# Local attention with a routed feed-forward layer on one core: weighing and joining moved behind the next scores

## The chip, the core and the metric

The kernel runs on one core of a Trainium2 chip. The core has five engines that run their own instruction streams in order and meet at semaphores: TensorE (matrix products; the profile calls its matmuls PE and its weight loads PEld), VectorE (DVE), ScalarE (ACT), GpSimd (POOL) and SyncE (SP, which here issues DMAs). TensorE writes to PSUM[...]; VectorE and ScalarE read it from there.

The metric is the device time of one launch in microseconds (us). Before the change it is 582.45 us, the median of three runs (581.14 to 582.88).

## The reference

The input x is 2 sequences of 2048 tokens with 256 channels. One block is computed:

```python
x = L0_attn_x                                            # (2, 2048, 256)
x = _layernorm(x + _L0_attn_ref(x, W_attn, b_attn, W_proj, b_proj))
x = _layernorm(x + _L0_ffn_ref(x, Wr, W1, b1, Wo, bo, gamma, beta))
```

The attention has 16 heads of 16 channels; a token sees itself and the 64 tokens before it (scores of other tokens are minus infinity), then softmax, weighted values, and the projection W_proj. The feed-forward part sends each token to the one of 8 experts with the largest router logit (`argmax` of softmax(x @ Wr.T)), computes gelu(x @ W1[e] + b1[e]) with 1024 hidden units, multiplies by the shared Wo, adds bo and x, and normalises with gamma and beta.

## The kernel before

The 4096 tokens are 32 tiles of 128. Four tiles make a chunk of 512, whose q, k and v are projected together. The kernel has two stages: the attention with the routing (one loop over 32 tiles, and an epilogue), and then blocks of 128 tokens of one expert each, gathered by indirect DMA, with a weight matrix of 1 MB per block.

The order of the work is written out by hand: `manual_schedule` keeps on every engine the order in which the Python code issues instructions. The loop is a software pipeline. In iteration i four tiles are in work: t = i, u = i - 1, w = i - 2 and z = i - 3.

- `scores(t)` (L533, L545): the mask and 64 small matmuls per tile, into four PSUM banks s0 to s3 that exist once each. The scores of the next tile therefore wait until the exponentials of this tile have read their bank.
- `row_max(t, r)` (VectorE, L557) and `exps(t, r)` (ScalarE, L561, four instructions) for each bank r.
- `fold(t, pair)` (GpSimd, L573, L581), `inverse` (VectorE, L589, L594), `spread_inverse` (GpSimd, L602): the sums of the softmax and their reciprocals.
- `turn(u, r)` (TensorE, L616): the probabilities are transposed, 128x128 four times per r. `keep_turned` copies them to SBUF, r = 0 and 2 on ScalarE (L622), r = 1 and 3 on VectorE (L624).
- `weigh(u)` (TensorE, L636, 64 narrow matmuls): the weighted values. `keep_weighed` (ScalarE, L646) copies them.
- `turn_inverse(w)` (TensorE, L655) and `normalise(w)` (VectorE, L659).
- `join(w)`: the output projection (TensorE, L667), the sum with the residual (VectorE, L673) and its statistics (L676, L677). `norm_scale(z)` (GpSimd, L683, L684) and `norm(z)` (VectorE, L692, which also stores the result) finish the first layer norm. `turn_x1`, `keep_x1` (L705, L710), `route` (L717, L722) and `turn_logits` (L727, L728) compute the router's logits, once per four tiles.
- Two slots per iteration hold the projections of later chunks: `project` (TensorE, L422, L426, L433) and `keep` (ScalarE L469, L475, L489; VectorE L471, L480, L483, L494, L499). By the slots the tiles are of some kinds. Tiles 6, 10, 14, 18, 22 transpose x and project q; 5, 9, ..., 25 project q and k with ScalarE draining both; 7, 11, ... hold k, v and the routing; 8, 12, ... a transposition of x and v. In the light tiles 1, 3 and 26 to 28 each slot is half a projection, and from tile 29 the first slot is empty; there the second exponentials come behind the second copy of turned probabilities.

PSUM has three pools. The score banks are one. The second, `turned`, has two buffers that alternate over all calls of `turn`, `turn_inverse`, `turn_x1`, `join`, `route`, `turn_logits`, `rank` and `table`: each waits until the one two calls earlier has been read. The third, `psum`, has two buffers for projections and weighted values.

The order of the parts in one iteration before the change, on TensorE: scores(t), turn(u, 0), turn(u, 1), first slot, turn(u, 2), turn(u, 3), second slot, turn_inverse(w), weigh(u), turn_x1(z), join(w). On ScalarE: copy of turn 0, exps 0 and 1, copy of turn 2, the first slot's copy, exps 2, the second slot's copy, exps 3, keep_weighed, keep_x1.

Small VectorE operations that sort tokens into lots (`hot`, `rank`, `places`) and that list the first blocks (`first_blocks`) are spread over iterations through the dictionary `early`. `full` marks iterations in which they are issued ahead of the first slot's projection.

Of the kernel before, what the change touches and what calls it, by code (L numbers as in the profile page):

```python
# [21 lines left out]
TPC = CH // P  # L22
NEG = -1.0e30
GAP = 64
SPLIT = (0, 8, 16, 28, 32)
PIECES = 8
WARM = 16
EARLY = 2
# [5 lines left out]
def kernel(  # L34
# [19 lines left out]
    KC = C // P  # L54
# [237 lines left out]
    with ExitStack() as att:  # L292
# [32 lines left out]
        def load_rest():  # L325
            nc.sync.dma_start(out=wpj, in_=w_proj.rearrange("(k p) f -> p k f", p=P))
            nc.sync.dma_start(out=bp_bc, in_=b_proj.partition_broadcast(P))
# [112 lines left out]
        def prepare(c, piece):  # L440

            first = c % (TPB // TPC) == 0
            if piece == 0:
                axT[c] = p2.tile([P, KC, CH], F32, tag="xT", name=f"xT_{c}")
            elif piece == 1:
                qs[c] = p2.tile([P, KC, 2, CH], F32, tag="q", name=f"q_{c}")
            elif piece == 2:
                ks[c] = p2.tile([P, KC, CTX + CH], F32, tag="k", name=f"k_{c}")
                if first:
                    nc.gpsimd.memset(ks[c][:, :, 0:CTX], 0.0)  # L450
                else:
                    nc.gpsimd.tensor_copy(ks[c][:, :, 0:CTX], ks[c - 1][:, :, CH : CH + CTX])
            else:

                vs[c] = values[c % 2]
                if c < 2:
                    nc.gpsimd.memset(
                        vs[c][:, :, :, 1, :].rearrange("p j m d -> p (j m) d"), 0.0
                    )

                vh[c] = p2.tile([P, TPC, NH // 2, 3, HD], F32, tag="h", name=f"h_{c}")
                if first:
                    nc.gpsimd.memset(vh[c][0:CTX, 0].rearrange("p m s d -> p (m s d)"), 0.0)
# [194 lines left out]
        def normalise(i):  # L658
            nc.vector.tensor_tensor(avs[i], avs[i], rTs.pop(i)[:, 0:KC, :], ALU.mult)  # L659

        def join(i):
            c, j = divmod(i, TPC)
            av = avs.pop(i)
            py = turned(f"py_{i}")
            py = py.rearrange("p a b -> p (a b)")
            for k in range(KC):
                nc.tensor.matmul(  # L667
                    py[:, 0:C], lhsT=av[:, k, :], rhs=wpj[:, k, :],
                    start=(k == 0), stop=(k == KC - 1),
                )  # L670

            s = xbs[c][:, j, :]
            nc.vector.tensor_tensor(s, py[:, 0:C], s, ALU.add)  # L673
            st = small.tile([P, 6], F32, tag="st", name=f"st_{i}")
            mv = small.tile([P, 2], F32, tag="mv", name=f"mv_{i}")
            nc.vector.bn_stats(st, s)  # L676
            nc.vector.bn_aggr(mv, st)  # L677
            norms[i] = mv
# [444 lines left out]
        xts[1] = load_x(1)  # L1123
        for n in range(3):
            prepare(0, n)
            for part in range(2):
                project(0, n, part)
                keep(0, n, part)
            if n == 0:
                load_rest()  # L1130

        def quick_sums(i, r):

# [53 lines left out]
        def put(at, *call, to=plan):  # L1187
            to.setdefault(at, []).append(partial(*call))


        for n, (t0, t1) in enumerate(lots[:EARLY]):
            at = t1 + 4
            put(at, some, ("hot", n), 3, to=early)
            put(at + 1, rest, ("hot", n), to=early)
            put(at + 2, rank, n, to=early)
            put(at + 2, some, ("places", n), 1, to=early)
            put(at + 3, some, ("places", n), 3, to=early)
            put(at + 4, rest, ("places", n), to=early)
            for t in range(t0, t1, 2):
                spread[at + 5 + (t - t0) // 2] = [partial(one_hots, nc.gpsimd, t)]  # L1200
        for n, count in enumerate((1, 4, 4, 4, 3)):
            put(SPLIT[EARLY] + 8 + n, some, "first", count, to=early)
        put(SPLIT[EARLY] + 13, rest, "first", to=early)
        for n in range(4 * (NT - 27)):
# [3 lines left out]
        for i in range(NT):  # L1208
# [4 lines left out]
            if w is not None:  # L1213
                inverse(w)
            scores(t)
            if z is not None and z > 0 and z % TPC == 0:
                route(z // TPC - 1)
            row_max(t, 0)
            if i == 0:
                consts = routing_constants()  # L1220
                for r in range(1, 4):
                    row_max(t, r)
                for r in range(2):
                    exps(t, r)
                for n in ((0, 3), (1, 0), (1, 1)):
                    prepare(*n)
                for part in ((0, 3, 0), (0, 3, 1), (1, 0, 0), (1, 0, 1)):
                    project(*part)
                    keep(*part)
                add_bias(0)  # L1230
                xts[2] = load_x(2)
                for r in range(2, 4):
                    exps(t, r)
                for part in parts[:2]:
                    project(*part)
                    keep(*part)
                for pair in range(2):
                    fold(t, pair)
                continue
            if i == 3:  # L1240
                turn_router()
            if u is not None:
                turn(u, 0)
                keep_turned(u, 0)
                turn(u, 1)
            if z is not None:
                norm_scale(z)
            if w is not None:
                spread_inverse(w)
            for part in slots:  # L1250
# [1 line left out]
                    prepare(*part[:2])  # L1252
            exps(t, 0)
            row_max(t, 1)
            if u is not None:
                keep_turned(u, 1)


            full = slots[0] and slots[1] and slots[0][1] > 0 and slots[0][3] == (0, 1)
            full = full or i == SPLIT[EARLY] + 8 or i >= NT - 4  # L1260
            if full:
                for task in early.get(i, ()):
                    task()
# [35 lines left out]
            exps(t, 2)  # L1299
            if slots[1]:  # L1300
                project(*slots[1][:4])
            if w is not None:
                turn_inverse(w)
                normalise(w)
            if t == NT - 1:
                for b in range(2):
                    gather(b)
# [7 lines left out]
                keep(*slots[1][:4])  # L1315
            elif slots[1] and slots[1][3][-1] == 1:
                keep(*slots[1][:3])
            if u is not None:
                weigh(u)
            exps(t, 3)  # L1320
            if t < NT - 1:
                fold(t, 1)
            if u is not None:
                keep_weighed(u)
            if i == NT - 2:
                table(0)
            if z is not None:
                turn_x1(z)
                keep_x1(z)

            if i == TPC:
                load_experts()
            if i == 2 * TPC:
                turn_biases()
            for task in plan.get(i, ()):
                task()
            if t == NT - 1:
                quick_sums(t, 1)
            if w is not None:
                join(w)  # L1340

        u, w, z = NT - 1, NT - 2, NT - 3
        lot = len(lots) - 2
        tiles = list(range(*lots[lot]))
        norm_scale(z)
        for n in range(4 * (NT - 27), 3 * PIECES):
            load_weights(n // PIECES, n % PIECES)
# [15 lines left out]
        first_layer(0, range(2, 4))  # L1365
        norm(z)
        join(w)
        norm_scale(w)
        for b in range(2, 4):
            gather(b)  # L1370
# [14 lines left out]
        first_layer(0, range(6, 8))  # L1385
        gelus(0, 1)
        join(u)
        norm_scale(u)
        first_layer(1, range(0, 2))
        turn_x1(w)  # L1390
# [33 lines left out]
    at = NFULL  # L1424
# [162 lines left out]
```

## Time and profile before

| what | value |
|---|---|
| median of three runs | 582.45 us |
| the profiled execution: time / span in the profile | 582.51 us / 580.7 us |
| granted TensorE clock, mean | 0.989 |
| first scores begin (L533) | 14.82 us |
| scores of tile 31 begin | 298.59 us |
| TensorE busy | 555.6 us |
| ScalarE busy | 302.0 us |
| VectorE busy | 398.6 us |

From the start of one tile's scores to the next it takes 8.4 to 10.3 us: tile 17 starts at 171.69, 18 at 181.60, 19 at 190.01, 20 at 200.28, 21 at 208.71; tile 26 at 255.29, 27 at 263.07, 28 at 271.71, 29 at 281.47, 30 at 290.12. From about 320 us on only the expert blocks run.

How to read it: a row of the timeline gives the start in us from the beginning of the span, the length, the engine, the line of the kernel, the operation, what it writes and reads, the sizes and how many equal instructions were merged into the row. In brackets stands how long the engine was idle before it and what ended that. A row of the stretches gives begin and end, length, and the busy time of each engine with the number of instructions. The end of a matmul is modelled, so starts are the firmer numbers.

### The profile page before, as it was taken

Reading aid. Unit: us, or ns where it says so; the run is one execution under the profiler, and the core shown is the slowest. Engines: PE = TensorE matmul, PEld = TensorE weight load, DVE = VectorE, ACT = ScalarE, POOL = GpSimd, SP = SyncE. Lnnn points to the kernel's source line nnn. Section 1 sums busy time; section 2 is a strip of 40 time slices with the busy share of each in tenths; the row PEclk is TensorE's granted clock in tenths of the full one; section 3 lists DMA queues with packets and bytes.
Section 4 is the critical chain, followed back from the end, with each engine's and each line's share of the span. In section 5 each row is a group of like instructions: output and inputs, shape, how many; then the busy total and the mean of one; then the engine's idle time right before and its main releaser. Section 6 shows DMA issues by size and latency. Waiting matters only on the chain. (4 is left out here: it accounts for less than half of the span.)

```text
span 580.7 us, 18514 instructions
## 1 busy us (share of the span) xinstructions
PE 555.6 (96%) x7312; PEld 453.3 (78%) x7312; DVE 398.6 (69%) x966; ACT 302.0 (52%) x1005; POOL 408.9 (70%) x603
## 2 busy tenths in 40 slices
PE   8999999999999999999898999999999999999991
PEld 4667677676776776766666899899999999999980
DVE  5658788788988788889877567887864232242483
ACT  2476675767758586676765433233335445445200
POOL 5358778577787877879873488887879777642484
PEclk9989999999999999999999999999999999999996
DMA  5301603012021220201334455555555757754010
GB/s 163 86 2 45 179 11 111 22 45 78 12 73 43 56 76 12 65 21 58 91 105 128 165 183 173 183 183 182 182 191 191 247 193 245 241 180 155 19 39 28
DMA packets 35605, 64.79 MB, mean 112 GB/s; under 512 B 8558, under 2 KB 23484, under 8 KB 35516
## 3 DMA queue, kind: packets, MB, share of 16 engines
q1 hardware_dynamic: 32444, 55.19, 29.4%
q0 software_dynamic: 3072, 8.39, 4.4%
q8 instruction: 59, 0.97, 0.7%
q14 instruction: 30, 0.25, 0.1%
HBM read 48.93 MB, written 8.39 MB: 99 GB/s over the span
## 5 line engine op out<-in xcount | busy, mean ns | idle before, releaser
L561 ACT ACTIVATE pr<-s,nm 128x128 f32<-128x128 f32 x512 | 142.4, 412 | 4.7 <-DVE nm L557 3.7
L573 POOL TENSOR_TENSOR fd<-pr 128x512 f32<-128x512 f32 x62 | 79.1, 1275 | 63.4 <-ACT pr L561 63.4
L233 ACT ACTIVATE gT<-ph,bc 128x128 f32<-128x128 f32 x200 | 57.2, 370 | 107.5 <-issue 65.6
L222 PEld LDWEIGHTS ph<-xgT,wb 128*128 128x128 f32 x800 | 93.5, 192 | 1.3
L222 PE MATMUL ph<-xgT,wb 128*128 128x128 f32 x800 | 94.4, 275 | 0.0
L242 PE MATMUL py<-wo_sb,gT 128*128 128x256 f32 x400 | 90.6, 380 | 0.0
L557 DVE TENSOR_REDUCE nm<-s 128x4 f32<-128x512 f32 x128 | 82.0, 680 | 5.9 <-PE s L545 5.5
L581 POOL TENSOR_TENSOR fd<-fd 128x512 f32<-128x512 f32 (+2 forms) x93 | 76.3, 821 | 7.3
L242 PEld LDWEIGHTS py<-wo_sb,gT 128*128 128x128 f32 x400 | 74.1, 190 | 9.0
L622 ACT COPY pT<-pt 128x512 f32<-128x512 f32 x64 | 38.4, 600 | 69.6 <-DVE nm L557 30.5
L616 PE MATMUL pt<-ident,pr 128*128 128x128 f32 x512 | 72.9, 284 | 1.7 <-ACT pT L622 0.6
L616 PEld LDWEIGHTS pt<-ident,pr 128*128 128x128 f32 x512 | 56.7, 143 | 18.3 <-issue 9.7
L426 PE MATMUL pj<-xT,wa 128*128 128x512 f32 x128 | 60.6, 595 | 0.8 <-issue 0.8
L264 DVE TENSOR_TENSOR y<-py,xbo 128x256 f32<-128x256 f32 x32 | 13.5, 422 | 53.2 <-PE py L242 53.2
L624 DVE COPY pT<-pt 128x512 f32<-128x512 f32 x64 | 43.7, 682 | 7.4 <-PE pt L616 7.3
L545 PEld LDWEIGHTS s<-k,q 32*64 32x64 f32 x2048 | 30.8, 130 | 15.6 <-issue 15.0
L222 PE MATMUL ph<-xpT,wb 128*128 128x128 f32 x352 | 40.8, 275 | 0.0
L222 PEld LDWEIGHTS ph<-xpT,wb 128*128 128x128 f32 x352 | 40.1, 192 | 0.1
L545 PE MATMUL s<-k,q 32*64 32x128 f32 x2048 | 38.8, 278 | 0.4 <-DVE k L494 0.4
L274 DVE TENSOR_SCALAR res<-y,mv_c,rs_c 128x256 f32<-128x256 f32 x32 | 16.0, 500 | 29.1 <-POOL rs_c L256 26.7
L426 PEld LDWEIGHTS pj<-xT,wa 128*128 128x128 f32 x128 | 21.7, 190 | 17.4 <-issue 14.3
L255 POOL TENSOR_TENSOR rs_b<-mv_b,eps_ffn 128x1 f32<-128x1 f32 x32 | 9.3, 290 | 37.0 <-DVE mv_b L253 30.6
(235 smaller groups left out, 1003.1 us busy)
## 6 DMA issues: line engine op xcount, KB each, us to landing
wb<-in_L_ffn_W_dram SPq DMA_DIRECT2D x33, 1024.0 KB
h<-v SPq DMA_DIRECT2D x24, 192.0 KB
xt<-in_L_attn_x_dram SPq DMA_DIRECT2D x8, 512.0 KB
x_d<-x SPq DMA_DIRECT2D x32, 128.0 KB
wb<-in_L_ffn_W_dram SPq DMA_DIRECT2D x24, 128.0 KB
h<-v SPq DMA_DIRECT2D x14, 96.0 KB
wo_sb<-in_L_ffn_Wo_dram SPq DMA_DIRECT2D x1, 1024.0 KB
wa<-in_L_attn_W_attn_dram SPq DMA_DIRECT2D x3, 256.0 KB
```

The costliest lines, as they stand in the source:

```text
L222: nc.tensor.matmul(phs[b, h][:, f % (NF // 2), :], lhsT=wb[:, k, ts(f, P)], rhs=xT[:, k, :], start=(k == 0), stop=(k == KC - 1),)
L233: nc.scalar.activation(gT[:, f, :], ph[:, f % (NF // 2), :], AF.Gelu, bias=bcs[b][:, f : f + 1], scale=1.0,)
L242: nc.tensor.matmul(py[:, 0:C], lhsT=gT[:, f, :], rhs=wo_sb[:, f, :], start=(f == 0), stop=(f == NF - 1),)
L426: nc.tensor.matmul(pm, lhsT=wa[:, k, ts(f, P)], rhs=axT[c][:, k, :], start=(k == 0), stop=(k == KC - 1),)
L545: nc.tensor.matmul(banks[i][r][a * CTX : (a + 1) * CTX, 2 * g + o, :], lhsT=qs[c][rows, g, o, t0 : t0 + CTX], rhs=ks[c][rows, g, t0 : t0 + P],
L557: nc.vector.tensor_reduce(maxes[i][:, r, :], banks[i][r], AX.X, ALU.max, negate=True)
L561: nc.scalar.activation(probs[i][:, r, x, :], banks[i][r][:, x, :], AF.Exp, bias=maxes[i][:, r, x : x + 1], scale=1.0,)
L573: nc.gpsimd.tensor_tensor(fd[:, 8 * pair : 8 * pair + 8, :], pr[:, two, :, 0:CTX].rearrange("p r x c -> p (r x) c"), pr[:, two, :, CTX:P]. ...
L581: nc.gpsimd.tensor_tensor(fd[:, :, 0:n], fd[:, :, 0:n], fd[:, :, n : 2 * n], ALU.add)
L616: nc.tensor.transpose(pt[:, x, :], probs[i][:, r, x, :], ident)
L622: nc.scalar.copy(pTs[i][:, r], pt)
L624: nc.vector.tensor_copy(pTs[i][:, r], pt)
```

## The change

`join` is cut in two: `join` keeps the projection on TensorE, and the new `join_sum` holds the sum and the statistics. In an iteration `weigh(w)` and `join(z)` stand directly behind `scores(t)`; weigh was for tile u at the end of the iteration before, join for tile w. `keep_weighed(w)`, `join_sum(z)` and `norm_scale(z)` stand behind `exps(t, 0)` and `row_max(t, 1)`. The first exponentials of a tile come ahead of the copies of turned probabilities. `turn_inverse` and `normalise` come behind the last exponentials. The start interleaves the first projection's two halves, the exponentials of tile 0 are regrouped, the biases' transposition stands earlier in iteration 8, and the small operations for lots and first blocks are placed otherwise.

```diff
@@ join
-
+            pts[i] = py
+
+        def join_sum(i):
+
+            c, j = divmod(i, TPC)
+            py = pts.pop(i)
             s = xbs[c][:, j, :]
             nc.vector.tensor_tensor(s, py[:, 0:C], s, ALU.add)
@@ start
         for n in range(3):
             prepare(0, n)
+        for part in range(2):
+            project(0, 0, part)
+            keep(0, 0, part)
+        load_rest()
+        for k in range(KC):
             for part in range(2):
-                project(0, n, part)
-                keep(0, n, part)
-            if n == 0:
-                load_rest()
+                project(0, 1, part, (k,))
+        for part in range(2):
+            keep(0, 1, part)
+        for part in range(2):
+            project(0, 2, part)
+            keep(0, 2, part)
@@ places of the lots
-            put(at + 3, some, ("places", n), 3, to=early)
-            put(at + 4, rest, ("places", n), to=early)
+            put(at + 3, rest, ("places", n), to=early)
...
-        for n, count in enumerate((1, 4, 4, 4, 3)):
+        for n, count in enumerate((0, 4, 4, 4, 4)):
@@ loop
             scores(t)
+            if w is not None:
+                weigh(w)
+            if z is not None:
+                join(z)
...
-                for r in range(2):
+                for r in range(3):
                     exps(t, r)
...
-                for r in range(2, 4):
-                    exps(t, r)
+                exps(t, 3)
...
                 turn(u, 0)
-                keep_turned(u, 0)
                 turn(u, 1)
-            if z is not None:
-                norm_scale(z)
...
             exps(t, 0)
             row_max(t, 1)
+            if w is not None:
+                keep_weighed(w)
+            if z is not None:
+                join_sum(z)
+                norm_scale(z)
             if u is not None:
+                keep_turned(u, 0)
                 keep_turned(u, 1)
-            full = full or i == SPLIT[EARLY] + 8 or i >= NT - 4
+            full = full or i >= NT - 4
...
-            if w is not None:
-                turn_inverse(w)
-                normalise(w)
...
-            if u is not None:
-                weigh(u)
             exps(t, 3)
             if t < NT - 1:
                 fold(t, 1)
-            if u is not None:
-                keep_weighed(u)
+            if i == 2 * TPC:
+                turn_biases()
             if i == NT - 2:
                 table(0)
+            if w is not None:
+                turn_inverse(w)
+                normalise(w)
...
-            if i == 2 * TPC:
-                turn_biases()
...
-            if w is not None:
-                join(w)
@@ epilogue
+        weigh(w)
+        keep_weighed(w)
+        join(z)
+        join_sum(z)
         norm_scale(z)
...
         join(w)
+        join_sum(w)
...
         join(u)
+        join_sum(u)
```

## The prediction

> **What bounds the kernel now.** I read the page first, then the attention stage cut at the starts of its tiles, then the timeline of one tile on TensorE, ScalarE and VectorE, and last the single waits of TensorE.
>
> ```profile
> PE 555.6 (96%) x7312; PEld 453.3 (78%) x7312; DVE 398.6 (69%) x966; ACT 302.0 (52%) x1005; POOL 408.9 (70%) x603
> ```
>
> The matmul row is full, the weight loads are not. The stretches below are four tiles each (span us, then busy us of PE, PEld, DVE, ACT, POOL):
>
> ```profile
> 97.54:134.14 36.60, 36.60 (x682) 26.32 (x683) 30.56 (x63) 25.35 (x84) 26.21 (x35) 1.00 0.17 51
> 171.69:208.71 37.02, 36.67 (x684) 26.32 (x683) 31.65 (x69) 25.45 (x84) 30.66 (x43) 1.00 0.17 52
> ```
>
> PE has no hole here; ACT works 6.4 us of a tile's 9.2. A rule speaks against taking PE for the bound: the Trainium skill, "Trainium Kernel Development and Optimization", Performance Expectations, says that matmul busy time measures badly how near a kernel is to its limit, because matmuls are pipelined, and to go by the weight loads. By those, (36.60 - 26.32)/4 = 2.6 us of each tile would be free, and the 1.9 us of matmuls that the change moves would fit in at no cost. The starts decide against it: the four matmuls of L426 below take 185.72 to 187.43, 0.43 each, back to back, with one 0.19 us weight load each. The array streams 512 columns meanwhile. I take PE as full.
>
> PE, tile 18 (start, length):
>
> ```profile
> 182.14 1.21 PE L545 MATMUL s<-k,q 32*64 32x128 f32 x64
> 183.28 1.09 PE L616 MATMUL pt<-ident,pr 128*128 128x128 f32 x8
> 184.21 0.60 PE L422 MATMUL pj<-ident,xt 128*128 128x128 f32 x4
> 184.65 1.22 PE L616 MATMUL pt<-ident,pr 128*128 128x128 f32 x8
> 185.72 1.88 PE L426 MATMUL pj<-xT,wa 128*128 128x512 f32 x4
> 187.43 0.38 PE L655 MATMUL pr<-ident,rw 128*128 128x128 f32 x2
> 187.75 0.43 PE L636 MATMUL pa<-pT,h 128*32 128x64 f32 x16
> 188.78 0.44 PE L705 MATMUL px<-ident,x 128*128 128x128 f32 x2
> 189.05 1.03 PE L667 MATMUL py<-wpj,av 128*128 128x256 f32 x4
> 190.01 0.61 PE L533 MATMUL s<-m_b,m_a 64*128 64x512 bf16 x4
> ```
>
> ACT, the same tile:
>
> ```profile
> 184.01 0.59 ACT L622 COPY pT<-pt 128x512 f32<-128x512 f32 x1 [2.39 <-issue]
> 184.50 2.18 ACT L561 ACTIVATE pr<-s,nm 128x128 f32<-128x128 f32 x8
> 186.51 0.65 ACT L622 COPY pT<-pt 128x512 f32<-128x512 f32 x1
> 186.97 0.67 ACT L469 COPY xT<-pj 128x512 f32<-128x512 f32 x1
> 187.45 2.27 ACT L561 ACTIVATE pr<-s,nm 128x128 f32<-128x128 f32 x8
> 189.46 0.52 ACT L646 COPY av<-pa 128x256 f32<-128x256 f32 x1
> ```
>
> The last exponential ends at 189.72, and the next scores, which overwrite its bank (each of the four score banks exists once), begin at 190.01: 0.29 us of slack. In tile 17 it is 0.52 (181.08 against 181.60), in tile 26 nothing (263.09 against 263.07). So there is a second ring beside PE: scores, row maxima, exponentials between copies, scores. What hides its end is L636, L705 and L667 (187.75 to 190.01), PE work behind the last projection. In tile 2 the ring already shows:
>
> ```profile
> 32.92 1.21 ACT L561 ACTIVATE pr<-s,nm 128x128 f32<-128x128 f32 x4
> 34.18 0.37 PE L533 MATMUL s<-m_b,m_a 64*128 64x512 bf16 x1 [1.24 <-ACT pr L561]
> ```
>
> **The change part by part.** Steps, from these rows: L636 with its change of shape 1.03 (187.75 to 188.78); L667 0.86 (four starts 0.216 apart); a batch of four exponentials 1.0 (184.50 to 186.51 for two); copies 0.48 (L622, L469), L646 0.3, q 0.67 and k 0.57 (tile 17: 177.59, 178.26, 179.26, 179.83). A turned score block is copied 0.73 after its first transposition starts (183.28, 184.01).
>
> *PE order.* L636 and L667 (1.03 + 0.86 = 1.89 us) go from the end of the tile to just behind the scores, one tile later. No PE work is added. In steady tiles a switch of matmul shape goes: the first L636 follows the last L655 by 0.203 where a transposition follows its own kind by 0.109, so a switch is 0.094. The order was scores, turn, ..., L655, narrow L636, L705, L667; now L636 stands between two other shapes, and four switches are left of five, except where routing follows. The Trainium skill, "TensorEngine Tiling (Array Packing)", Key Properties, says that changing the tiling mode drains the engine, which speaks for the change: counted alone, 22 tiles x 0.094 = -2.1 us. But the row tells what such a drain is worth only while PE is the bound; where the ring binds it is nothing.
>
> *ACT ring.* The copy of the turned block now waits for turns that stand 1.89 later; ahead of it go exponentials (1.0) and L646 (0.3), in time that was idle (the 2.39 above). When the ring binds, I count from the start of the last L533, R: scores end 1.44 later (34.18 to 35.62), row maximum 0.68, so exponentials from 2.15 to 3.15, L646 to 3.45; turn from 1.44 + 1.03 + 0.86 = 3.33, its copy 4.05 to 4.53. From there by kind of tile:
> - Tiles 6, 10, ... 22 (transposition of x first): exponentials to 5.55, second copy 6.07, xT 6.55, two batches 8.55, 0.2 of tail and 0.05 to the release: 8.8. Before 8.41 to 8.63, so +0.4 or +0.2; five tiles +1.5.
> - Tiles 5, 9, ... 25 (q, then k): the second turn stands behind a 1.72 projection, at 6.17; copy 6.87 to 7.35, q 8.02, exponentials 9.02, k 9.6, last batch 10.6: 10.85. Before 9.49, and 9.9 in tiles 13 and 17: four at +1.36 and two at +0.95, +7.3.
> - Tiles 8 to 24 by fours, and the routing tiles 7 to 23: 8.4 and 10.15 against 8.42 (8.6 to 9.3 in some) and 10.27: -1.1 in all. Here the switch counts, and so does tile 8, where the turn of the biases cost a 0.4 us wait for L710 at L667 that its new place avoids.
> - Light tiles, whose second exponentials come after the second copy: 26: turn at 5.31, copy 6.01 to 6.48, three batches, 9.73 against 7.78. 27 has the routing copy ahead: 10.83 against 8.65. 28: 9.73 against 9.76, which holds 1.0 of waits. 29 and 30: 9.85 (marks on VectorE ahead of the third maximum, 1.5) and 9.1, against 8.65 and 8.47. Sum +6.0.
> - Tiles 1 to 4: 9.0 against 8.43; 8.1 against 9.47 (no join yet); 9.73 against 8.0; 8.4 against 8.43: +0.9.
> Sum of the ring: 1.5 + 7.3 - 1.1 + 6.0 + 0.9 = +14.6.
>
> *A new wait of PE.* The join's PSUM tile shares its buffer with the second turn, which now waits for the sum:
>
> ```profile
> 190.12 0.42 DVE L673 TENSOR_TENSOR xb<-py,xb 128x256 f32<-128x256 f32 x1 [0.16 <-PE py L667]
> ```
>
> From the first L667 to the end of this sum is 190.54 - 189.05 = 1.49; the second turn would start 0.86 + 0.44 = 1.30 after it: about 0.25 of wait with the release. Queued behind it are the projections and the second turn; it is contained in the ring times above, and alone would cost 22 x 0.25 = 5.5 us.
>
> *VectorE* has the sum and its statistics behind two row maxima; GpSimd's norm_scale (0.75) follows later, ahead of a fold that waits for ACT anyway: nothing. But VectorE ends the tiles of the third kind with v, normalise and inverse, which I place 0.25 to 0.35 past the time at which the next row maximum could start, in some 11 tiles: 0 to 3.3 us. I take 1.5.
>
> *Start.* The first projections are interleaved by k:
>
> ```profile
> 9.60 0.78 ACT L475 ACTIVATE q<-pj,bq,half 128x512 f32<-128x512 f32 x1 [2.95 <-PE pj L426]
> 11.28 0.30 PEld L426 LDWEIGHTS pj<-xT,wa 128*128 128x128 f32 x2 [0.83 <-DVE q L483]
> ```
>
> The built order still has the first matmul wait for both copies of x, so it starts no sooner; the first q is complete after six of eight passes, not four, and L475, L483 and the next projection, which needs its buffer, slip by 2 x 0.43: +0.9. The exponentials moved ahead of the copy of xT lie under PE: nothing.
>
> *End.* Behind the last scores stand two more joins and one more weighing on PE, and the routing copy ahead of the exponentials; the turn of tile 31 begins 11.4 after the scores by the same steps against 10.2 (298.59 to 308.79), +1.2. The load of weights keeps its issue places on SyncE; the expert blocks after 330 us are PE alone and only shift.
>
> *Lots and first blocks.* The same small VectorE operations, 0.16 to 0.5 each. In tiles 15 and 23 three more stand ahead of the logits and third maximum, about 0.5, covered there by the second turn to 0.2: inside the rounding.
>
> Sum: 14.6 + 1.5 + 0.9 + 1.2 = +18.2 on 582.5, the profiled execution's time (580.7 of span and 1.8 around it), which is the median: **600.6 us**.
>
> **The rivals.**
> 1. *The ring as worked*, 592 to 607. For it: tile 26 at zero slack, tile 2's wait. Chance 0.77.
> 2. *The ring half hidden*: exponentials or copies overlap more, and PE's 0.25 waits set the loss: 5.5 + 0.9 - 2.1 = +4.3, or +8 with half of the q-and-k tiles' 7.3: 587 to 591. Against it: ACT's starts are regular. 0.10.
> 3. *VectorE binds as well*: 27 tiles late by another 0.3, up to 0.4 with the early tasks in series: 608 to 612. VectorE is busy 31 of 37 us, so possible. 0.06.
> 4. *Faster*: ACT follows in its slack, PE stays the bound. Then -2.1 of switches, -1.2 at tile 2's scores, -2.5 of the waits for q, x1T and rw, +0.9: 577.6. It decides if the chain from the first copy takes under about 4.1 us in tiles 6, 10, ..., where I count 4.7 (4.05 to 8.75); a batch would have to take 0.8, and the rows show 1.0. 0.05.
> 5. *No change*: small gains against the small waits, within 0.3%. The built order shows that the moves do take place on every engine, so not for want of effect. 0.02.
>
> **How the numbers follow.** 0.3% (1.7 us) is about what this measurement can tell. Slower: 0.77 + 0.10 + 0.06 = 0.93; faster 0.05, same 0.02. The range 588 to 607 leaves out most of cases 3 to 5 and the lower part of 2.
>
> **What would show it.** In the profile after: L533 waiting for ACT pr L561 in most tiles, some 0.3 to 2 us each and longest in tiles 5, 9, ... and 26, 27; PE busy about the same in us, its share down to about 93%; waits of L616 for the sum near 0.25; the first scores 0.9 later; from the first expert block on the same durations. Wrong, if L533 has no such waits or tiles of the q-and-k kind stay under 10 us.

## The result and the profile after

The changed kernel takes 618.97 us, the median of four runs (615.94 to 623.26), beside 582.41 us for the kernel before on the same chip: a ratio of 1.0645, 95% interval 1.0617 to 1.0673. It is slower, as forecast, but by 36.6 us where 18.2 were forecast, and it lies above the range that was given (588 to 607).

The profiled execution took 623.26 us, 621.5 of it span, against 580.7 before. The busy row of the page, then four tiles each (9 to 12 and 17 to 20, cut at the first L545 of a tile, where the prediction cuts at the first L533; after the length come the busy times of PE, PEld, DVE, ACT and POOL, then the granted clock):

```profile
PE 574.3 (92%) x7311; PEld 460.5 (74%) x7312; DVE 395.9 (64%) x966; ACT 304.6 (49%) x1005; POOL 408.8 (66%) x603
```

```profile
109.41:149.21 39.80, 38.20 (x684) 26.68 (x682) 28.65 (x59) 25.71 (x84) 26.41 (x35) 1.00 0.15 46
190.35:230.15 39.80, 38.20 (x684) 26.68 (x682) 29.02 (x64) 25.71 (x84) 30.81 (x43) 1.00 0.17 48
```

No engine has more to do in a steady group of tiles: ACT 25.7 against 25.4 us, DVE some 2 us less. But four tiles take 39.80 instead of 36.6 to 37.0, and PE, which was without a hole, is idle for 1.60 of them. The other 1.5 us or so are recorded as PE busy, because the modelled end of a matmul covers short waits. The list of TensorE's single waits (total us, times, longest) names two that the kernel before had in one place or not at all:

```profile
PE px L710 <- DVE x L697: 10.0, 19, 1.8
PE s L533 <- ACT pr L561: 7.0, 13, 1.2
...
PE pa L636 <- issue: 1.3, 1, 1.3
...
PE px L710 <- DVE b1T L1111: 0.8, 1, 0.8
```

The second line is the ring that the prediction was built on: scores waiting for exponentials. The first is one that it did not have: the transposition of x1 (L710; L705 before), the last TensorE work ahead of the next scores, waits for VectorE's `norm` (L697). Tile 18, which the prediction showed of before, on TensorE after (start, length):

```profile
200.97 0.37 PE L533 MATMUL s<-m_b,m_a 64*128 64x512 bf16 x1 [0.43 <-ACT pr L561]
201.27 1.21 PE L545 MATMUL s<-k,q 32*64 32x128 f32 x64
...
203.44 1.13 PE L667 MATMUL py<-wpj,av 128*128 128x256 f32 x4
204.40 1.34 PE L616 MATMUL pt<-ident,pr 128*128 128x128 f32 x8
205.58 0.60 PE L422 MATMUL pj<-ident,xt 128*128 128x128 f32 x4
206.01 1.17 PE L616 MATMUL pt<-ident,pr 128*128 128x128 f32 x8
...
208.74 0.38 PE L655 MATMUL pr<-ident,rw 128*128 128x128 f32 x2
208.95 0.38 PE L710 MATMUL px<-ident,x 128*128 128x128 f32 x2
209.27 0.95 PE L533 MATMUL s<-m_b,m_a 64*128 64x512 bf16 x4
210.15 0.91 PE L545 MATMUL s<-k,q 32*64 32x128 f32 x43
```

and on ScalarE:

```profile
203.20 1.14 ACT L561 ACTIVATE pr<-s,nm 128x128 f32<-128x128 f32 x4 [2.02 <-DVE nm L557]
204.21 0.39 ACT L646 COPY av<-pa 128x256 f32<-128x256 f32 x1
205.09 0.59 ACT L622 COPY pT<-pt 128x512 f32<-128x512 f32 x1 [0.50 <-PE pt L616]
205.58 1.14 ACT L561 ACTIVATE pr<-s,nm 128x128 f32<-128x128 f32 x4
206.65 0.58 ACT L622 COPY pT<-pt 128x512 f32<-128x512 f32 x1
207.13 0.59 ACT L469 COPY xT<-pj 128x512 f32<-128x512 f32 x1
207.61 2.19 ACT L561 ACTIVATE pr<-s,nm 128x128 f32<-128x128 f32 x8
```

The ring is to be read from the copy at 205.09 on: copy, exponentials, copy, xT, eight exponentials, with no idle bracket between them, ending at 209.80. The four L533 at 209.27 spread over 0.88 (209.27 to 210.15; 0.54 before, 190.01 to 190.55), and the tile takes 8.88, where the prediction worked out 8.8. L710 follows L655 here without a wait, 0.22 from start to start. Of the 1.34 in the L616 row 0.25 is the second turn's wait for the sum (205.58 - 204.40 = 1.18 to the projection behind it; 0.93 before, 183.28 to 184.21). No bracket shows it, but in tile 20 below the sum ends at 224.70 and the second turn's first transposition starts at 224.76.

Tile 20 is of the third kind, for which no loss was forecast. TensorE from its second projection on, and VectorE in the same tile:

```profile
226.76 1.89 PE L433 MATMUL pj<-wa,xT 128*128 128x256 f32 x8
228.49 0.38 PE L655 MATMUL pr<-ident,rw 128*128 128x128 f32 x2
229.27 0.41 PE L710 MATMUL px<-ident,x 128*128 128x128 f32 x2 [0.40 <-DVE top L787]
229.61 0.61 PE L533 MATMUL s<-m_b,m_a 64*128 64x512 bf16 x4
```

```profile
224.28 0.42 DVE L678 TENSOR_TENSOR xb<-py,xb 128x256 f32<-128x256 f32 x1 [0.90 <-PE py L667]
224.74 0.43 DVE L681 BATCH_NORM_STATS2 st<-xb 128x6 f32<-128x256 f32 x1
225.20 0.18 DVE L682 BATCH_NORM_AGGREGATE mv<-st 128x2 f32<-128x6 f32 x1
225.52 0.69 DVE L624 COPY pT<-pt 128x512 f32<-128x512 f32 x1
226.12 1.28 DVE L557 TENSOR_REDUCE nm<-s 128x4 f32<-128x512 f32 x2
227.32 0.68 DVE L624 COPY pT<-pt 128x512 f32<-128x512 f32 x1
227.92 0.68 DVE L471 COPY xT<-pj 128x512 f32<-128x512 f32 x1
228.52 0.61 DVE L697 TENSOR_SCALAR x<-xb,mv,rs 128x256 f32<-128x256 f32 x1
```

VectorE runs from the join's sum (224.28) to the norm (229.13) with next to no gap; 0.14 after its end L710 starts. (The bracket names `top`, which ends at 229.26; I take the norm, since it writes what L710 reads, and the distance is 0.14 in tile 19 too, where the norm is named.) All of it now lies in one tile: scores, weigh, join, sum, second turn, its copy, two row maxima, another copy, xT, norm, turn of x1, next scores. Before, the sum belonged to the end of the tile ahead. This is a third chain beside PE's work and ScalarE's ring.

The whole difference of the spans by kind of tile, in us, each from the starts of L545 before and after:

| part | predicted | measured |
|---|---|---|
| start, to tile 0's scores | +0.9 | +0.9 |
| tiles 1 to 4 | +0.9 | +5.4 |
| q and k: 5, 9, ... 25 | +7.3 | +9.1 |
| transposition of x first: 6, 10, ... 22 | +1.5 | +2.3 |
| third kind and routing: 8, 12, ... 24 and 7, 11, ... 23 | -1.1 | +7.7 |
| light tiles 26 to 30 | +6.0 | +9.1 |
| end, from tile 31 on | +1.2 | +6.4 |
| VectorE, in 11 tiles | +1.5 | in the rows above |
| sum | +18.2 | +40.8 |

The measured column is of the profiled execution, the slowest of the four; the median is 4.3 us below it. The part on the hardware at the end says why.

### The profile page after: what moved, and what is told of

It reads as the page before. It is cut to its first block, busy times and chain, and to the rows that moved or that the text cites. A ratio compares the mean times of both kernels' runs of the same rounds, so it can differ in the third digit from the quotient of the medians.

```text
span 621.5 us, 18504 instructions
## 1 busy us (share of the span) xinstructions
PE 574.3 (92%) x7311; PEld 460.5 (74%) x7312; DVE 395.9 (64%) x966; ACT 304.6 (49%) x1005; POOL 408.8 (66%) x603
## 5 line engine op out<-in xcount | busy, mean ns | idle before, releaser
L616 PE MATMUL pt<-ident,pr 128*128 128x128 f32 x512 | 75.7, 281 | 4.1 <-DVE xb L678 1.0
L616 PEld LDWEIGHTS pt<-ident,pr 128*128 128x128 f32 x512 | 58.0, 142 | 24.1 <-DVE xb L678 9.5
L624 DVE COPY pT<-pt 128x512 f32<-128x512 f32 x64 | 44.0, 688 | 14.1 <-PE pt L616 11.6
L545 PEld LDWEIGHTS s<-k,q 32*64 32x64 f32 x2048 | 32.3, 136 | 24.3 <-issue 23.4
L545 PE MATMUL s<-k,q 32*64 32x128 f32 x2048 | 40.9, 289 | 0.6 <-DVE k L494 0.6
L222 PE MATMUL ph<-xpT,wb 128*128 128x128 f32 x352 | 40.8, 275 | 0.0
L667 PE MATMUL py<-wpj,av 128*128 128x256 f32 x128 | 37.4, 416 | 0.8 <-DVE av L659 0.5
```

The costliest lines, as they stand in the source:

```text
L222: nc.tensor.matmul(phs[b, h][:, f % (NF // 2), :], lhsT=wb[:, k, ts(f, P)], rhs=xT[:, k, :], start=(k == 0), stop=(k == KC - 1),)
L545: nc.tensor.matmul(banks[i][r][a * CTX : (a + 1) * CTX, 2 * g + o, :], lhsT=qs[c][rows, g, o, t0 : t0 + CTX], rhs=ks[c][rows, g, t0 : t0 + P],
L616: nc.tensor.transpose(pt[:, x, :], probs[i][:, r, x, :], ident)
L624: nc.vector.tensor_copy(pTs[i][:, r], pt)
```

## The experiments

Ratios are to the kernel before on the same chip. The diffs are against the changed kernel, unless said otherwise.

**Undoing the moves on TensorE.** First both, with the first exponentials left ahead of the copies:

```diff
@@ loop
             scores(t)
-            if w is not None:
-                weigh(w)
-            if z is not None:
-                join(z)
...
+            if w is not None:
+                turn_inverse(w)
+                normalise(w)
...
+            if u is not None:
+                weigh(u)
             exps(t, 3)
...
+            if w is not None:
+                join(w)
+                join_sum(w)
```

> The changed kernel with weigh, join and the turn of the inverses back at their old places; the interleaved start, the exponentials ahead of copies, the biases' turn and the lots' places stay changed. If the moved TensorE work makes the loss: within 2 us of the kernel before (581 to 585), the start alone +0.9. If the small edits or the order on ScalarE make a good part of it: 590 or more.

Measured: 599.79 us, 1.0312 [1.0293, 1.0331]. So 19 us of the loss go with the moves, and 18 stay without them. The list of TensorE's waits says where those are:

```profile
PE pt L616 <- ACT pT L622: 16.4, 18, 1.4
```

The third turn overwrites the PSUM buffer of the first, and the first one's copy now stands behind four exponentials that wait for a row maximum. With the turns back at 1.1 us behind the start of L545, the copy comes too late in tiles with a short first slot (0.93 in the tile below):

```profile
133.20 1.09 PE L616 MATMUL pt<-ident,pr 128*128 128x128 f32 x8
134.13 0.60 PE L422 MATMUL pj<-ident,xt 128*128 128x128 f32 x4
135.66 1.09 PE L616 MATMUL pt<-ident,pr 128*128 128x128 f32 x8 [0.93 <-ACT pT L622]
```

Then one move at a time, each with the turn of the inverses at its old place: `weigh` alone back (the join stays behind the scores), and the join alone back (`weigh` stays).

> The changed kernel with weigh back at the end of its tile (and the turn of the inverses where it was); join stays behind the scores. The ring through ScalarE starts 0.9 us later instead of 1.9, and weigh covers both its end and the wait of L710 for the norm: 588 to 596. If the join's own wait (second turn behind the sum) is what costs, it stays near 610; if only weigh's place matters, it falls to 583.

> The changed kernel with join and its sum back at the end of the tile; weigh stays behind the scores. The turns are 1.0 us later, no wait for the sum, join covers the end: 584 to 592 if the two rings (exponentials, and sum to norm to L710) make the loss. Near 610 if weigh's place alone matters.

Measured: 595.83 us, 1.0247 [1.0224, 1.0270], and 613.0 us, 1.0539 [1.0491, 1.0587]. From 599.8 with neither, the join alone takes off 4.0 us, since its 0.96 ahead of the turns covers most of the wait for the copy (16.4 us in 18 places become 1.4 in 2); `weigh` alone adds 13.2, some of it half clock (its executions have a mean clock of 0.978 to 0.987, those with neither 0.990 to 0.992); both together add 19.2. `weigh` is the expensive one. With `weigh` back, a steady tile has no bracket on TensorE and yet takes 8.72 (tile 18) against 8.41. The row of its first two turns shows 0.28 of it:

```profile
190.33 1.37 PE L616 MATMUL pt<-ident,pr 128*128 128x128 f32 x8
191.54 0.60 PE L422 MATMUL pj<-ident,xt 128*128 128x128 f32 x4
```

1.21 to the projection, 0.93 before: the new wait for the sum, at the price that the prediction gave it (0.25).

**The other order on ScalarE.** The copy of the first turn goes back ahead of the first exponentials, with both moves left in:

```diff
                 turn(u, 0)
+                keep_turned(u, 0)
                 turn(u, 1)
...
             if u is not None:
-                keep_turned(u, 0)
                 keep_turned(u, 1)
```

> The changed kernel with the copy of the first turned block ahead of the first exponentials again. If the ring through ScalarE binds, the exponentials wait for turns that stand behind weigh and join: about 0.7 us more in the some 17 tiles bound by it, 625 to 635. If ScalarE's order is itself the harm, it gets faster than the changed kernel, below 615.

Measured: 624.82 us, 1.0743 [1.0715, 1.0772], at the lower end of what was expected if the ring binds. Here ScalarE has nothing to do while it waits for the later turns, and the exponentials follow behind:

```profile
PE px L710 <- DVE x L697: 12.8, 21, 1.8
PE s L533 <- ACT pr L561: 10.5, 20, 1.2
```

**Everything of the order back.** Both of these undone; what stays is the interleaved start with the regrouped exponentials of tile 0, the biases' turn, the places of the lots and `norm_scale` behind row maximum 1 (`x_both_back` and `x_copy_first` together).

> The changed kernel with weigh, join, the turn of the inverses and the order of the first copy and first exponentials all as before; the interleaved start, the biases' turn, the lots' places and norm_scale behind the first exponentials stay. If the exponentials ahead of the copy made the 18 us that stayed when only the TensorE work went back: 582 to 584 (start +0.9). If the small edits made them: near 599.

Measured: 581.78 us, 1.0001 [0.9994, 1.0008], from 21 runs. The small edits together are worth nothing. In its profile the first scores are late as in the changed kernel, and tile 8 gives 0.44 back (8.84 against 9.28). Tile 2 takes 8.24 against 9.70, but that is the clock: the profile of the kernel before has a stretch at half clock there (at 35.8 us) and this one has none. The four corners:

| | copies first | exponentials first |
|---|---|---|
| weigh and join at the old places | 581.8 | 599.8 |
| weigh and join behind the scores | 624.8 | 619.0 |

The two halves do not add. Each is a loss alone (18.0 and 43.0), and together they cost 37.2. I take it that the exponentials, when they come first, fill time that the later turns leave idle on ScalarE (the 2.02 in the first of its rows above).

**Is it VectorE's norm?** If the wait of L710 costs what the list says, an earlier norm must give it back. It goes directly behind row maximum 2:

```diff
             row_max(t, 2)
+            if z is not None:
+                norm(z)
             if slots[0]:
...
-            if z is not None:
-                norm(z)
             exps(t, 2)
```

> The changed kernel with the norm of tile z on VectorE directly behind the third row maximum, ahead of the fourth, the last copy of turned probabilities and the drains of projections. If the second ring (join, sum, norm, L710, next scores) costs the 10 us that L710 waits for the norm in the changed kernel's profile: those waits vanish and the time falls by 4 to 9 us, to 610 to 615. If only the ring through the exponentials decides, the wait moves to L533 and the time stays within 2 us of 619.

Measured: 618.38 us, 1.0641 [1.0605, 1.0676]: no gain. The wait is gone from the list, and two others have taken its place:

```profile
PE s L533 <- ACT pr L561: 10.4, 15, 1.2
PE px L710 <- DVE pT L624: 5.9, 18, 0.9
```

The tile that L710 writes shares its PSUM buffer with the fourth turn, which VectorE copies (L624). The norm now runs ahead of that copy and makes it later. So not the place of the norm holds L710, but what VectorE has to do between the sum and the end of the tile.

**Taking L710 out of that chain.** The turn of x1 goes one tile later, directly behind `weigh`:

```diff
                 weigh(w)
+            if z is not None and z > 0:
+                turn_x1(z - 1)
+                keep_x1(z - 1)
...
-            if z is not None:
-                turn_x1(z)
-                keep_x1(z)
-
```

> The changed kernel with the turn of x1 (L710 there) one tile later, behind weigh, so that the norm on VectorE has most of a tile's time. If the waits of L710 for VectorE stand alone on the path: 5 to 9 us less, 610 to 614. If the exponentials' ring and VectorE's other work end at the same time: within 3 us of 619, the wait shown at L533 or L667 instead.

Measured: 616.04 us, 1.0602 [1.0582, 1.0622], 3 us less. No wait of L710 for the norm is left, and tiles 12, 16, 24 take 8.82 instead of 9.21, four of the five routing tiles 10.41 instead of 10.79. But the turn of x1 now stands ahead of the turns of the probabilities and so makes ScalarE's ring longer, and the scores wait there:

```profile
PE s L533 <- ACT pr L561: 16.4, 22, 1.2
```

```profile
194.05 0.60 PE L533 MATMUL s<-m_b,m_a 64*128 64x512 bf16 x3
195.75 0.37 PE L533 MATMUL s<-m_b,m_a 64*128 64x512 bf16 x1 [1.09 <-ACT pr L561]
```

This is a q-and-k tile: 11.10, where the changed kernel takes 10.92. Tiles 6, 10 and 18 take 9.25 instead of 8.88. What VectorE gives back in one kind of tile, the longer ring takes in the other, so the 3 us are not the whole worth of L710's waits.

**Shortening ScalarE's ring.** The exponentials of the fourth bank become one instruction over 512 columns, with the maximum of one head for all four (so the softmax of three heads in four has another offset, and the output is not the reference's). Once in the changed kernel, once in the kernel before:

```diff
         def exps(i, r):
+            if r == 3:
+                nc.scalar.activation(
+                    probs[i][:, r], banks[i][r], AF.Exp, bias=maxes[i][:, r, 0:1], scale=1.0,
+                )
+                return
```

> The changed kernel with the four exponentials of the fourth bank as one instruction with the first head's maximum for all four: the output is not the reference's, the flow of data is. ScalarE gets about 0.5 us shorter per tile. If the ring through the exponentials binds in some 17 tiles: 7 to 9 us less, 610 to 612, and the waits of L533 shrink. If VectorE's ring or TensorE's own order binds everywhere: within 2 us of 619.

> The kernel before with the same shortened exponentials (the output is not the reference's). TensorE bounds it, so nothing is gained but tile 2's wait and tile 26: 580.5 to 582. If ScalarE were near the bound there too, it would gain 5 us or more.

Measured: 613.03 us, 1.0530 [1.0494, 1.0567], and 580.58 us, 0.9986 [0.9979, 0.9993]. Six us come off the changed kernel and one off the one before. ScalarE's ring is worth about six times as much after as before; yet it does not hold the whole loss, since the other wait stays (in this kernel the lines of the code are five higher, so L715 and L702 are L710 and L697; of L533's waits 1.3 us more stand under L566, the other exponentials):

```profile
PE px L715 <- DVE x L702: 10.2, 19, 1.8
...
PE s L533 <- ACT pr L561: 1.4, 4, 0.8
```

The tiles show which chain holds which. Tiles 9, 17 and 21 (q and k) go from 10.92 to about 10.47, tiles 6, 10 and 18 from 8.88 to 8.53, tile 26 from 9.85 to 9.40: there the ring is the bound. Tiles 12, 16 and 20 stay at 9.21 and the routing tiles at 10.79, to a hundredth or two: there it is not.

At the same mean clock (0.988 to 0.991) the single executions compare so: 615.9 and 616.2 us for the changed kernel, 616.5 and 616.8 with the norm early, 614.0 with the turn of x1 later, 611.3 twice with the shorter exponentials. So the gains are none, 2 and 5 us, with little of the half clock in them.

**Are the half-clock stretches the cause?** (They are shown in the last part.) At the ends of iterations 3 and 27 to 31, 50 transpositions that nobody reads keep TensorE busy:

```diff
+        def fill(i, count):
+
+            ready[i] = psum(f"pa_{i}")
+            for n in range(count):
+                nc.tensor.transpose(ready[i][:, 0:P], ident, ident)
...
+            if i in FILL:
+                fill(u, FILL[i])
```

> The changed kernel with 48 to 50 transpositions more that nobody reads, 8 each at the end of iterations 3 and 27 to 30 and 10 at the end of 31, put where TensorE waits. They keep TensorE busy. If the stretches at half clock that only the changed kernel's profile shows (57, 303, 333 and 344 us) cost time, they vanish and it falls by 4 to 8 us in spite of the added work, and its runs spread less. If the clock is a symptom only: within 2 us of 619, or slower.

Measured: 619.09 us, 1.0651 [1.0629, 1.0673]. The four stretches are gone from its profile, and its runs lie closer together (618.68 to 620.85, against 615.94 to 623.26). Tiles 4 and 28 are shorter by 1.55 and 1.26 (9.21 and 10.77), the part behind the start of tile 31 by 2.8. The median stays: the 50 transpositions themselves are up to 5.4 us of TensorE work (50 x 0.109), and in this profile the weighing also waits 1.5 us in tile 5 and 0.9 behind the last scores (the next run has more on such waits). So the stretches explain the spread and part of the loss, not the loss. `x_copy_first` says the same: its profile has no stretch at half clock between the first scores and the last expert block, and it is the slowest version.

The changed kernel once more:

> The changed kernel itself, profiled once more. Its four times spread from 615.9 to 623.3, and the profile at 623.3 has stretches at half clock at 57, 303, 333 and 344 us. If those make the spread, an execution near 616 has fewer of them, and tiles 4 and 28 and the stretch after the last scores are shorter by about 1.5, 1.3 and 3 us where they are missing, with all other tiles the same. If the spread comes from elsewhere (DMA), the difference lies in other tiles.

Measured: 620.17 us, 1.0661 [1.0599, 1.0723], from two runs. The profiled execution (621.57 us, mean clock 0.978) is again one with stretches, so the question was not answered by it; tiles 4 and 28 in `x_fill` answer it in part. The stretches begin within 0.1 us of the same places (56.8, 302.5, 333.3 and 343.5 us). Tile 4 again takes 10.76, tile 28 12.32 (12.03 in the first profile). Tile 8 takes 10.59 instead of 11.49: the last of its L636 waits 0.45 us, in the first profile 1.34. So the size of that wait changes from execution to execution. The profile names nothing that it waits for. In all eight such waits of 0.45 us and more within the weighing, in six of these profiles, TensorE goes on 1.3 to 1.7 us after the end of a packet of DMA queue 8, which the profile calls `instruction` (99.83 and 101.49 here, 98.95 and 100.43 in `z_again`, 67.74 and 69.18 in `x_fill`). So it may be the loading of the program; no run was made to try it.

**What is usable of it.** `y_moves_back` suggests that the kernel before loses a little by the order of GpSimd's `spread_inverse` and `norm_scale` and at the biases' turn. Against the kernel before:

```diff
-            if z is not None:
-                norm_scale(z)
             if w is not None:
                 spread_inverse(w)
+            if z is not None:
+                norm_scale(z)
...
                 project(*slots[1][:4])
+            if i == 2 * TPC:
+                turn_biases()
...
-            if i == 2 * TPC:
-                turn_biases()
```

> The kernel before with two small changes: on GpSimd the spread of the inverses ahead of norm_scale (0.75 us earlier for L655, which waits 1.2 us for it in tiles 28 and 29), and the biases' turn ahead of the turn of the inverses in iteration 8 (0.4 us of L667). 1.0 to 1.6 us faster than before, 580 to 581.5, if those waits are on TensorE's path; no change otherwise.

Measured: 581.19 us, 0.9990 [0.9982, 0.9999], from 13 runs. That is 0.6 us less than the kernel before, the only version that beats both with the computation kept whole, and little more than the measurement can tell. The wait of L655 is gone, but L636 now waits 1.3 us for a copy on VectorE in the same tiles 28 and 29; tile 8 gains 0.5, tile 24 loses 0.55.

## Why the prediction was right in sign and wrong in size

**What held.** *PE full, so the change cannot win by idle PE time*: the moved work had no free TensorE time to go to, and no version with it was faster. *The switch of shape* is saved at its size: L710 follows L655 0.22 later in tile 18, where L636 followed it 0.31 later. *The start*: +0.9, measured 15.78 to 16.64, but sure to half a microsecond only, since two other kernels with the old start have 16.15 and 16.34. *The ring through ScalarE* is there, and the two kinds of tile worked out on it came out within a tenth: 10.92 in three of the six q-and-k tiles against 10.85 worked out, 8.88 in three of the five with the transposition of x first against 8.8; all of these six tiles are among those that the shorter exponentials shorten. *Light tiles 26 and 27* took 9.85 and 10.90 against 9.73 and 10.83. What was named as its sign, L533 waiting for the exponentials, is in the list, in 13 places rather than in most tiles. *VectorE's chain* was seen, as the term "I take 1.5" and as rival 3.

**The step that failed: "Tiles 8 to 24 by fours, and the routing tiles 7 to 23: 8.4 and 10.15 ... -1.1 in all."** They took 9.21 and 10.79 and lost 7.7 us. The prediction counted TensorE's work there and put the waits of TensorE for VectorE at nothing. In tile 20 the 0.79 over 8.42 are these terms:

- +0.25, the second turn's wait for the sum (224.07 to 225.25 is 1.18, before 0.93). The prediction had this wait at its right size, and then wrote that it is contained in the ring times. That holds where the ring binds. In these tiles it took the ring to be no bound and counted PE's work, and there the wait counts in full. This was an error inside its own working. `x_weigh_back` shows it by itself, in tiles where TensorE waits for no ring.
- +0.57, L710's wait for the norm (from L655 to L710 228.49 to 229.27 is 0.78; without a wait, in tile 18, 0.22). The prediction looked at what VectorE does at the end of the tile and asked whether the next row maximum would be late. It did not follow the sum, once moved, through everything that VectorE does behind it to the norm, and from there to L710, which is the last TensorE work ahead of the scores.
- minus 0.09, the saved switch of shape (0.22 where it was 0.31, from L655 to the next matmul), as counted, but it falls into the wait for the norm and so gains nothing here. The rule from "TensorEngine Tiling (Array Packing)", Key Properties, that a change of tiling mode drains the engine, agrees with the 0.203 against 0.109 of the prediction's rows.
- +0.07, a gap that the new order brings: L710 to L533 costs 0.34 where L705 to L667 cost 0.27.

Without the two waits the tile would have taken about 8.4, which is what the prediction has. In the routing tile 19 the 0.52 come out of the same rows: +0.45 for L710 (219.39 to 220.06 is 0.67), -0.09, +0.07, and +0.10 for the switch from the join to the routing (212.31 to 213.38 is 1.07, from the join to the scores before 0.96). The second turn loses nothing there, since the routing stands between it and the join.

The same step counted tile 8 as a gain, because the biases' turn in its new place would no longer hold up L667. It holds up L710 instead, for the copy of the biases (the last line of the waits after: 0.8 us, once); with the wait of 1.3 us at L636 among its terms, tile 8 alone makes 2.2 of the 7.7. In `y_moves_back`, with the old order around it, the new place does gain: 8.84 against 9.28.

**VectorE, "I take 1.5".** Its own bounds were 0 to 3.3, for another wait (the next row maximum) in some 11 tiles. L710's waits for the norm are 10.0 us in the profiled execution, of which 6.0 lie in tiles 25, 27, 28, 29 and 31 and the rest in 14 earlier tiles, so the upper end was too low as well. That VectorE's chain binds in other tiles than ScalarE's ring is what `x_short_after` shows tile by tile. The two attempts to take it away by another order gave 0.6 and 2.9 us (618.97 less each), not 10, since each put its load on a wait elsewhere.

**Tiles 1 to 4, "+0.9", measured +5.4.** About 1.5 us is half clock in tile 4 (10.76; with the stretch filled 9.21). Another 1.1 is a comparison of unlike things in tile 2. There the prediction set its 8.1 against the 9.47 of the profile before. But in that profile tile 2 stood at half clock for 3.4 us (from 35.8 us on), and it does so in the profile after too, where it took 9.40. At full clock tile 2 takes 8.24 in `y_spread_first`, with the old order, and 8.26 in `y_turn_late`, with the new one: the 1.4 us counted as a gain are not there. Tile 3 took 10.75 instead of 9.73. There the copy of the turned router weights (L336) stands ahead of the second row maximum on VectorE and waits for a TensorE instruction that the moves pushed behind the join: the second row maximum starts at 49.05, 1.8 after the end of the first, and the sum behind it makes the second turn wait 0.61. That copy was not in the working.

**Light tiles, "+6.0", measured +9.1.** Tiles 26 and 27 fit; 28 and 30 took 12.03 and 10.00 against 9.73 and 9.1. In tile 28 1.26 us are half clock. For the rest it is not the ring that binds from tile 28 on: L710 waits for VectorE there, 1.78, 1.46 and 1.53 us in tiles 28, 29 and 30. That tile 29 came out near (9.59 against 9.85) is luck.

**End, "+1.2", measured +6.4.** In the profile of `x_norm_early`, which has no half clock there, the part behind the start of tile 31 takes 283.7 us (614.9 - 331.19) against 281.6 before: +2.1. The other 4 us I put down to the half-clock stretches, which `x_fill` shows to be most of it (2.8 less without them, in spite of the added work).

**The rivals.** Rival 3 (VectorE binds as well, 608 to 612, chance 0.06) was nearest, and still 7 us too low. Rival 2 (the ring half hidden) fell with the L533 waits, 4 and 5 with the sign. "Faster" was to be decided by whether the chain from the first copy in tiles 6, 10, ... takes under 4.1 us where 4.7 were counted; in tile 18 it takes 4.71 (205.09 to 209.80).

**What stays open.** The half-clock stretches were removed only by adding work, so what the changed kernel would take without them is an estimate: 616 us, from the two of its runs in which the mean clock was 0.989. And no run takes VectorE's chain away without a change to another one.

## What to carry to other kernels

When a step is moved ahead in a software pipeline, follow its result, not only the step: through every instruction queued behind it on the engine that takes it up, to the last instruction ahead of the point where the loop closes, and ask this for each engine in turn. A wait that is hidden where a ring binds must be counted in each kind of iteration where it doesn't. If two rings end within a few tenths of each other, another order that removes the wait which the profile names can put the load on another wait, as twice here. Shortening one instruction of a ring instead shows, tile by tile, where that ring binds. And before a saving is read off a row, look whether the row stood at full clock.

## What the runs showed of the hardware that was not expected

Stretches of TensorE at half clock in the midst of a busy stage. The stretches of the changed kernel's profile (the third number from the end is the granted clock):

```profile
56.90:60.30 3.40, 3.40 (x98) 2.81 (x82) 1.29 (x2) 1.51 (x5) 3.16 (x5) 0.50 0.18 55
302.60:306.10 3.50, 2.87 (x98) 2.46 (x96) 2.65 (x6) 0.91 (x4) 3.34 (x5) 0.51 0.48 155
333.40:336.80 3.40, 3.40 (x118) 2.93 (x120) 1.24 (x2) 0.03 (x1) 3.17 (x5) 0.50 0.75 197
343.60:350.40 6.80, 6.26 (x78) 4.92 (x79) 3.93 (x12) 2.98 (x12) 0.91 (x3) 0.50 0.52 155
```

and the 3.4 us ahead of the first three of them, with one stretch more (the last) that no half clock follows:

```profile
53.50:56.90 3.40, 2.25 (x58) 1.16 (x63) 1.62 (x6) 2.56 (x10) 3.09 (x3) 1.00 0.52 133
299.20:302.60 3.40, 2.27 (x40) 0.86 (x38) 3.33 (x7) 2.62 (x11) 3.02 (x3) 1.00 0.13 40
330.00:333.40 3.40, 1.87 (x26) 1.01 (x25) 3.21 (x9) 2.77 (x11) 2.17 (x2) 1.00 0.12 40
309.50:312.90 3.40, 1.79 (x13) 1.40 (x11) 3.33 (x8) 3.09 (x12) 1.39 (x2) 1.00 0.01 2
```

The kernel before has one such stretch in its loop (at 35.8 us), where the changed kernel has one too. The Trainium skill, "TensorE: Matmul & The Clock Gate", Part 1, puts the half rate behind an idle window of about 3.4 us. The length agrees with these rows. But here TensorE was not idle for a window: in the 3.4 us ahead it was busy for 1.9 to 2.3, with several short waits for the two rings. Busy time alone does not decide it either: from 309.5 us on TensorE was busy for 1.79 of 3.4 us, and the clock stayed full. What decides is open. What `x_fill` shows is that the four stretches go when TensorE is kept busy ahead of them. So waits that add up to 1.1 to 1.5 us in 3.4 can cost their own length and then up to 1.7 us more (an estimate: half of a stretch of 3.4 us). In the executions of the changed kernel the span goes with the mean clock: 614.4 and 614.1 us at 0.989, 617.0 at 0.983, 619.8 to 621.5 at 0.977 and 0.978. With it goes the spread of 7 us, where the kernel before spreads over 2. The prediction had no term for it. As an estimate from these runs it makes up 3 of the 36.6 us (619 against 616), and 7 in the slowest run.
